# A four-direction scan block: both directions streamed side by side, the short convolution as banded matmuls on column tiles

## The chip, the cores and the metric

One NeuronCore of a Trainium2 chip runs the whole program. The metric is the device time of one execution in microseconds. TensorE (PE in the profile) multiplies, VectorE (DVE) and ScalarE (ACT) do elementwise work, GpSimd (POOL) does elementwise work on SBUF, and SyncE (SP) issues most DMAs.

## The reference

The input is 4 images of 128 channels and 96 x 96 pixels, float32. Each is group-normalised (32 groups of 4 channels, mean and variance over the whole image), read as a sequence of 9216 pixels in four orders (by lines forward and reversed, by columns forward and reversed), and each sequence goes through the same small network:

```python
t = _grouped1x1(x, in_proj_w, in_proj_b, G)          # 4 groups of 32 channels -> 128 each
u, gate = (t[:, :HID], t[:, HID:])                   # 256 channels each
u = jax.nn.silu(u)
u = lax.conv_general_dilated(u, dw_w, ..., feature_group_count=HID)   # 5 taps, per channel
s = _conv1x1(u, ssm_in_w)                            # 256 -> 32
a = DMIN + (DMAX - DMIN) * jax.nn.sigmoid(_conv1x1(u, ssm_delta_w, ssm_delta_b))
a = jnp.clip(a, 0.0001, 0.9999)
bb = jnp.tanh(_conv1x1(u, ssm_b_w, ssm_b_b))
cc = jnp.tanh(_conv1x1(u, ssm_c_w, ssm_c_b))
prefix = jnp.cumsum(jnp.log(a), axis=-1)
hst = jnp.exp(prefix) * jnp.cumsum(bb * s * jnp.exp(-prefix), axis=-1)  # h = a h + bb s
u = u + _conv1x1(cc * hst + ssm_d[None, :, None] * s, ssm_out_w)        # 32 -> 256
u = _grouped1x1(u * jax.nn.sigmoid(gate), mix_w, mix_b, G)
return _conv1x1(u, out_proj_w, out_proj_b)           # 256 -> 128
```

The four results go back to the pixel order, are fused by a 512-to-128 product, and the input is added. So 4 x 4 x 9216 = 147456 pixels pass through the network.

## The kernel before

All data is float32, channels on partitions, pixels along the free dimension. An image is read in a column order (V, from a transposed copy in memory) and then a line order (H): 8 phases. `xn` holds the normalised image of the phase, `sil` the activated first half of the input product for the whole image (two halves of 128 channels, two pixels of padding at each end), and `acc` the input plus all results so far. Mix, output and fuse products are folded at the start into one matrix per direction and half, `w_fin`.

A phase makes two passes over the image, one per direction; the reversed one takes the taps mirrored and the scan backwards. A pass has 20 chunks: 18 of 5 lines (480 pixels) and 2 of 3 lines (288). The main loop runs over 8 x 2 x 20 = 320 steps in program order, and each engine works through its own instructions in that order:

- `conv_and_gate` (lines 240 to 277): for the first 128 channels five matmuls with diagonal matrices (`diag`), accumulated in PSUM (`pc`); for the others one ACT copy with a scale and four DVE multiply-adds; then the gate's two matmuls on 32 rows each (`pg`) and their sigmoid.
- `ssm_out` of the step before (lines 321 to 331): two matmuls of 32 rows (`z` into `pc` and `pz`), and the product with the gate on DVE.
- `front` (lines 207 to 238) for a chunk of the next phase, in the second pass only: normalisation, two matmuls of 32 rows (`pu`), sigmoid, and the product that makes it a silu, stored in `sil`. So one front serves both passes.
- `scan` (lines 281 to 319): two matmuls (`pp`, 4 x 32 outputs: s, b, c, delta), three activations, two POOL operations on `a`, and DVE's product, scan and two more operations, all on 32 partitions.
- `accumulate` of the step before (lines 333 to 358): two matmuls (`py`) and the addition into `acc`; on the last pass of an image the chunk is written out and the next image's chunk is loaded into `acc`.

Statistics of the next image (`stats_chunk`, `stats_finish`) run in the first V pass. PSUM has 8 banks: two each for `ps_x` (front and gate), `ps_u`, `ps_p`, one each for `ps_z` and `ps_y`.

## Time and profile before

| | |
|---|---|
| times of three runs | 3605.2, 3606.55, 3615.43 us (median 3606.55) |
| the profiled execution | 3603.76 us, its span 3602.0 us |
| mean granted TensorE clock | 0.945 |
| instructions | 27637 |
| DMA | 92.14 MB, mean 26 GB/s |

The span runs from the first to the last instruction that the profiler recorded. In the views of the profile, PE is matmuls and PEld weight loads; a group is given by line, engine and operation, out<-in by the program's names, out and in as partitions x elements, the count, then busy us and mean ns of one, then the idle time of the engine just before and what released it. In a timeline a row is start (us), length (us), engine, line, operation and count of what is merged in it.

### The profile page before, as it was taken

The numbers are of one execution on the slowest core, as the hardware profiler recorded it, in microseconds if no ns is written. First come the engines' busy times: TensorE is split into PE (matmuls) and PEld (weight loads), VectorE is DVE, ScalarE is ACT, GpSimd is POOL, SyncE is SP. The second block draws the span as 40 slices with busy tenths as digits, with TensorE's granted clock in tenths as the row PEclk, the third lists the DMA queues.
The fourth block names the chain that finished last, engine by engine and source line by source line (L and its number), as shares of the span: only waits on it lengthen the run. The fifth ranks groups of instructions, "written<-read, shape, count | busy, mean of one in ns | idle before, by whom it ended". The sixth has DMA issues, their size and how long they took to land.

```text
span 3602.0 us, 27637 instructions
## 1 busy us (share of the span) xinstructions
PE 3501.1 (97%) x9032; PEld 1539.4 (43%) x9032; DVE 2877.5 (80%) x4442; ACT 1572.0 (44%) x2572; POOL 393.0 (11%) x653
## 2 busy tenths in 40 slices
PE   7999999999999999999999999999999999999999
PEld 3334444444444444444444444444444444444443
DVE  7888887788877888778887788777887788877777
ACT  3334444444444444344444444444444344444343
POOL 0011111111111111111111111111111111111111
PEclk7899999999999999999999999999999999999999
DMA  4210000011200000001110000000120000000000
GB/s 151 86 34 15 20 20 1 0 39 58 62 0 0 18 22 14 1 0 54 59 46 0 4 20 22 9 0 6 58 66 29 0 7 22 20 6 0 6 22 26
DMA packets 56625, 92.14 MB, mean 26 GB/s; under 512 B 7296, under 2 KB 56352, under 8 KB 56480
## 3 DMA queue, kind: packets, MB, share of 16 engines
q1 hardware_dynamic: 54720, 89.68, 8.2%
q8 instruction: 70, 1.15, 0.1%
q10 hardware_dynamic: 1760, 0.70, 0.1%
q14 instruction: 75, 0.61, 0.1%
HBM read 71.48 MB, written 18.87 MB: 25 GB/s over the span
## 4 chain that ended last, share of the span: by engine, by line
PE 44%; DVE 44%; issue 6%; ACT 4%; DMA 2%; ACTq 0%; POOL 0%; DVEq 0%; POOLq 0%
DVE u L261 12%; PE pc L248 11%; PE pc L324 8%; PE pp L287 8%; DVE h L308 7%; PE pz L328 6%; PE py L339 5%; DVE z L318 4%; DVE tb L302 4%; DVE z L317 4%; DVE gv L331 3%; DVE u L330 3%; PE pu L224 3%; PE pg L270 3%; ACT u L259 3%
## 5 line engine op out<-in xcount | busy, mean ns | idle before, releaser
L248 PE MATMUL pc<-sil,diag 128*128 128x480 f32 (+1 forms) x3200 | 1298.1, 552 | 0.0
L261 DVE SCALAR_TENSOR_TENSOR u<-sil,w_dw,u 128x480 f32<-128x480 f32 (+1 forms) x1280 | 889.0, 695 | 135.5 <-ACT u L259 124.0
L248 PEld LDWEIGHTS pc<-sil,diag 128*128 128x128 f32 x3200 | 609.9, 191 | 641.0 <-issue 623.0
L287 PE MATMUL pp<-u,w_proj 128*128 128x480 f32 (+1 forms) x1280 | 698.8, 674 | 2.8 <-DVE u L261 2.2
L264 ACT COPY u<-pc 128x480 f32<-128x480 f32 (+1 forms) x320 | 173.8, 543 | 1046.1 <-PE pc L248 1046.0
L339 PE MATMUL py<-gv,w_fin 128*128 128x480 f32 (+1 forms) x1280 | 588.9, 584 | 1.0
L300 POOL TENSOR_SCALAR a<-a 32x480 f32<-32x480 f32 (+1 forms) x320 | 190.9, 597 | 3173.1 <-ACT a L294 3173.1
L329 DVE TENSOR_TENSOR gv<-pc,gv 128x480 f32<-128x480 f32 (+1 forms) x320 | 204.0, 638 | 344.1 <-PE pc L324 335.5
L274 ACT ACTIVATE gv<-pg,b_in 128x480 f32<-128x480 f32 (+1 forms) x640 | 379.2, 642 | 143.3 <-PE pg L270 132.1
L287 PEld LDWEIGHTS pp<-u,w_proj 128*128 128x128 f32 x1280 | 247.0, 215 | 386.1 <-issue 269.5
L339 PEld LDWEIGHTS py<-gv,w_fin 128*128 128x128 f32 x1280 | 270.6, 213 | 311.5 <-issue 226.7
L324 PE MATMUL pc<-z,w_so 32*128 32x480 f32 (+1 forms) x640 | 332.1, 598 | 64.6 <-DVE z L318 62.7
L259 ACT ACTIVATE u<-sil,w_dw 128x480 f32<-128x480 f32 (+1 forms) x320 | 216.7, 677 | 382.2 <-DVE gv L331 376.3
L308 DVE TENSOR_TENSOR_SCAN h<-a,h,tb 32x480 f32<-32x480 f32 (+1 forms) x304 | 354.6, 1167 | 2.1 <-POOL a L301 1.0
L270 PE MATMUL pg<-xn,w_in 32*128 32x480 f32 (+1 forms) x1280 | 345.5, 600 | 0.6 <-ACT gv L274 0.6
L228 ACT ACTIVATE sg<-pu,b_in 128x480 f32<-128x480 f32 (+1 forms) x320 | 202.1, 639 | 258.9 <-PE pu L224 258.7
L328 PE MATMUL pz<-z,w_so 32*128 32x480 f32 (+1 forms) x640 | 300.8, 549 | 0.0
L292 ACT ACTIVATE tb<-pp,b_proj 32x480 f32<-32x480 f32 (+1 forms) x320 | 204.0, 637 | 142.3 <-PE pp L287 136.6
L224 PE MATMUL pu<-xn,w_in 32*128 32x480 f32 (+1 forms) x640 | 251.0, 625 | 10.2 <-DVE sil L231 7.9
L302 DVE TENSOR_TENSOR tb<-pp,tb 32x480 f32<-32x480 f32 (+1 forms) x320 | 199.1, 622 | 73.5 <-ACT z L298 71.6
L330 DVE TENSOR_TENSOR u<-pz,u 128x480 f32<-128x480 f32 (+1 forms) x320 | 203.9, 637 | 42.7 <-PE pz L328 2.1
L231 DVE SCALAR_TENSOR_TENSOR sil<-pu,b_in,sg 128x480 f32<-128x480 f32 (+1 forms) x320 | 219.5, 692 | 21.7 <-ACT sg L228 19.8
(54 smaller groups left out, 2050.0 us busy)
## 6 DMA issues: line engine op xcount, KB each, us to landing
xn<-in_xv SPq DMA_DIRECT2D x72, 240.0 KB, 2.6
acc<-in_xh SPq DMA_DIRECT2D x72, 240.0 KB, 2.8
xn<-in_xh SPq DMA_DIRECT2D x72, 240.0 KB, 2.6
out<-res SPq DMA_DIRECT2D x72, 240.0 KB, 2.0
xs<-in_xh SPq DMA_DIRECT2D x54, 240.0 KB, 2.6
xn<-in_xv SPq DMA_DIRECT2D x8, 144.0 KB, 2.3
acc<-in_xh SPq DMA_DIRECT2D x8, 144.0 KB, 2.3
xn<-in_xh SPq DMA_DIRECT2D x8, 144.0 KB, 2.1
```

The lines of the kernel that those rows point to most:

```text
L224: nc.tensor.matmul(pt[:, :n], w_in[q, :], xn[q, span(c)], start=True, stop=True)
L248: nc.tensor.matmul(pu[:, :n], diag[:, w, :], sil[:, 0, bass.ds(o + k, n)], start=(k == 0), stop=(k == K - 1),)
L259: nc.scalar.activation(u[:, 1, :n], src, AF.Copy, scale=coef)
L261: nc.vector.scalar_tensor_tensor(u[:, 1, :n], src, coef, u[:, 1, :n], ALU.mult, ALU.add)
L270: nc.tensor.matmul(pg[:, :n], w_in[q, :], xn[q, span(c)], start=True, stop=True)
L274: nc.scalar.activation(gv[:, j, :n], pgs[j][:, :n], AF.Sigmoid, bias=b_in[:, 2 + j : 3 + j])
L287: nc.tensor.matmul(pp[:, :n], w_proj[:, j, :], u[:, j, :n], start=(j == 1), stop=(j == 0))
L302: nc.vector.tensor_mul(tb[:, :n], s, tb[:, :n])
L308: nc.vector.tensor_tensor_scan(dirn(h), dirn(a), dirn(tb), 0.0 if st["first"] else carry[0], ALU.mult, ALU.add,)
L324: nc.tensor.matmul(pu[:, :n], w_so[:, 0:P], z[:, :n], start=False, stop=True, skip_group_check=True)
L328: nc.tensor.matmul(pz[:, :n], w_so[:, P:HID], z[:, :n], start=True, stop=True)
L339: nc.tensor.matmul(py[:, :n], w_fin[:, d, j, :], gv[:, j, :n], start=(j == 0), stop=(j == 1))
```

## The change

The layouts in memory change: `xs` holds the four sequences of each image already in their order, padded, and with every fourth pixel together (pixel 4n + q stands at [q, n]); `xr` holds the images in line order with the same split within a line, and so do `acc` and the output.

Both directions of a phase now advance together. A stretch is 16 lines (1536 pixels) of each direction's own sequence, and a unit is one of its four pixel phases p (384 pixels, every fourth one) of one direction s: 8 phases x 6 stretches x 4 x 2 = 384 units, with s alternating. `sil` for the whole image, `xn` and the normalised copy are gone: `wn` and `bn` carry the normalisation in weights and biases, front is computed anew for each direction, and only `x_in` (two input tiles) and a double-buffered `sil` per direction remain.

- `rows` does the front of one channel group g (32 channels of both halves, four pixel phases stacked on 4 x 32 partitions) eight units ahead, the gate of the unit eleven units back, and the product out of the scan (`pz`) for that unit; silu is one ACT operation, sigmoids become tanh with the halves moved into weights.
- `conv` contracts over 4 pixels x 32 channels: for each half, block k and group g a matmul of 128 rows and 32 columns with a banded matrix (`band`). DVE and the diagonal matmuls have no part in it any more.
- `proj` serves a pair of units (both directions of one p): call 0 gives b and delta, call 1 gives c and s, each for two directions on 4 x 32 columns; so the products, the scan (one of 1536 columns on 64 partitions per stretch) and the output products work on both directions at once.
- `accumulate` reverses the result of the second direction as it adds. After the last unit of a stretch, 16 lines of `acc` are written out and loaded with the next image.

Every matmul in these functions writes 32 columns (`mm`, column tile `col`). PSUM has four banks for `x` (front, gate, conv, `py`), two for `z`, one each for `p0` and `p1`.

```diff
-LINES = [5] * 18 + [3] * 2
...
+R = 4
+LN = 16
+NS = HH // LN
+N = LN * WW // R
+M = WW // R
+LAG = 11
+UB = 8
...
-    xn = big.tile([P, L], F32, name="xn")
-    sil = big.tile([P, 2, L + 2 * PAD], F32, name="sil")
+    x_in = [big.tile([P, R, N + 1], F32, name=f"x_in{s}") for s in range(2)]
...
+    phases = [
+        (b, order, dirs)
+        for b in range(B)
+        for order, dirs in (("V", ((0, 2), (1, 3))), ("H", ((2, 0), (3, 1))))
+    ]
...
+    def psx(name):
+        return ps.tile([P, 512], F32, tag="x", bufs=4, name=name)
...
+        wn = sp.tile([P, P], F32, tag="wn", name=f"wn_{b}")
+        nc.vector.tensor_scalar_mul(wn, w_in, norm[:, 1:2])
+        gm4 = sp.tile([P, 4], F32, tag="gm4", name=f"gm4_{b}")
+        nc.vector.tensor_scalar_mul(gm4, gmask, norm[:, 0:1])
+        pb = psx(f"pbn_{b}")
+        nc.tensor.matmul(pb[:, 0:4], wn, gm4, start=True, stop=True)
+        bn = sp.tile([P, 4], F32, tag="bnorm", name=f"bnorm_{b}")
+        nc.vector.tensor_sub(bn, b_in, pb[:, 0:4])
+        nc.vector.tensor_scalar_mul(bn[:, 2:4], bn[:, 2:4], 0.5)
+        bs = sp.tile([P, 2, 4], F32, tag="bsilu", name=f"bsilu_{b}")
+        for q in range(R):
+            for g in range(4):
+                nc.gpsimd.tensor_copy(
+                    bs[32 * q : 32 * q + 32, :, g], bn[32 * g : 32 * g + 32, 0:2]
+                )
+        stats[b] = (wn, bn, bs)
...
+    def load_front(step, s):
+        if step * UB < NU:
+            un = units[step * UB + s]
+            nc.sync.dma_start(
+                x_in[s][0:64, :, :],
+                xs[un["b"], un["lay"], 0:64, :, bass.ds(un["st"] * N, N + 1)],
+            )
+    def gate_at(un):
+        return (un["p"] + PAD) % R, (un["p"] + PAD) // R
+    def load_gate(i):
+        if i < NU:
+            un = units[i]
+            q, _ = gate_at(un)
+            nc.sync.dma_start(
+                x_in[un["s"]][64:P, q, :],
+                xs[un["b"], un["lay"], 64:P, q, bass.ds(un["st"] * N, N + 1)],
+            )
...
+        for q in range(R):
+            r = slice(32 * q, 32 * q + 32)
+            nc.gpsimd.tensor_copy(id32[r, :], ident[r, r])
+        for j in range(2):
+            for p in range(R):
+                for k in range(2):
+                    for g in range(4):
+                        m = R * k - p + R - 1
+                        nc.gpsimd.tensor_scalar_mul(
+                            band[:, j, p, k, g, :], id32, w_dw[:, j, g, m : m + 1]
+                        )
...
-                nc.vector.tensor_copy(w_fin[:, d, j, :], pt[:, :P])
+                nc.vector.tensor_scalar_mul(w_fin[:, d, j, :], pt[:, :P], 0.5)
...
-    def front(ph, c): ...
-    def conv_and_gate(st): ...
-    def scan(st): ...
-    def ssm_out(st): ...
-    def accumulate(st): ...
+    def mm(o, col, lhsT, rhs, start, stop):
+        r = slice(32 * col, 32 * col + 32)
+        nc.tensor.matmul(o[r, : rhs.shape[-1]], lhsT, rhs, start=start, stop=stop,
+                         skip_group_check=True)
+    sils = {}
+    def rows(i, bi):
+        front = gate = None
+        if i is not None:
+            step, k = divmod(i, UB)
+            s, g = divmod(k, 4)
+            un = units[step * UB + s]
+            wn, _, bsil = stats[un["b"]]
+            if g == 0:
+                sils[step, s] = wk.tile(
+                    [P, 2, 4, N + 1], F32, tag=f"sil{s}", name=f"sil_{step}_{s}"
+                )
+            sil = sils[step, s]
+            pf = [psx(f"pf_{i}_{j}") for j in range(2)]
+            front = (un, wn, bsil, s, g, sil, pf)
+        if bi is not None:
+            bu = units[bi]
+            gwn, gbn, _ = stats[bu["b"]]
+            pg = [psx(f"pg_{bu['id']}_{j}") for j in range(2)]
+            gate = (bu, gwn, gbn, pg)
+        for c in range(4):
+            if front:
+                for j in range(2):
+                    r = slice(32 * j, 32 * j + 32)
+                    mm(pf[j], c, wn[r, 32 * g : 32 * g + 32], x_in[s][r, c, :], True, True)
+            if gate:
+                q, off = gate_at(bu)
+                for j in range(2):
+                    r = slice(64 + 32 * j, 96 + 32 * j)
+                    mm(pg[j], c, gwn[r, 32 * c : 32 * c + 32],
+                       x_in[bu["s"]][r, q, off : off + N], True, True)
+        if gate:
+            pz = ps.tile([P, 2, 512], F32, tag="z", name=f"pz_{bu['id']}")
+            z = scans[bu["step"]][1]
+            for c in range(4):
+                for j in range(2):
+                    r = slice(64 * j + 32 * bu["s"], 64 * j + 32 * bu["s"] + 32)
+                    mm(pz[:, j, :], c, w_so[r, 128 * j + 32 * c : 128 * j + 32 * c + 32],
+                       z[r, bu["p"], :], True, True)
+        if front:
+            for j in range(2):
+                nc.scalar.activation(
+                    sil[:, j, g, :], pf[j][:, : N + 1], AF.Silu, bias=bsil[:, j, g : g + 1]
+                )
+            if g == 3:
+                if un["st"] == 0:
+                    nc.gpsimd.memset(sil[0:64, :, :, 0:1], 0.0)
+                if un["st"] == NS - 1:
+                    nc.gpsimd.memset(sil[64:P, :, :, N : N + 1], 0.0)
+                load_front(step + 1, s)
+        if gate:
+            gv = wk.tile([P, 2, N], F32, tag="gv", name=f"gv_{bu['id']}")
+            for j in range(2):
+                nc.scalar.activation(
+                    gv[:, j, :], pg[j][:, :N], AF.Tanh, bias=gbn[:, 2 + j : 3 + j], scale=0.5
+                )
+            load_gate(bi + UB)
+            u = bu["u"]
+            nc.vector.tensor_add(pz[:, :, :N], pz[:, :, :N], u)
+            nc.vector.scalar_tensor_tensor(gv, gv, 1.0, pz[:, :, :N], ALU.add, ALU.mult)
+            bu["v"] = gv
+    def conv(un, j):
+        sil = sils[un["step"], un["s"]]
+        if j == 0:
+            un["u"] = wk.tile([P, 2, N], F32, tag="u", bufs=LAG, name=f"u_{un['id']}")
+        pc = psx(f"pc_{un['id']}_{j}")
+        for k in range(2):
+            for g in range(4):
+                mm(pc, g, band[:, j, un["p"], k, g, :], sil[:, j, g, k : k + N], k == 0, k == 1)
+        nc.scalar.copy(un["u"][:, j, :], pc[:, :N])
+    scans = {}
+    qb, qc, qa, qs = (slice(MH * i, MH * (i + 1)) for i in range(4))
+    def proj(i, which):
+        un = units[i]
+        step, p = un["step"], un["p"]
+        if step not in scans:
+            scans[step] = [
+                wk.tile([P, N, R], F32, tag="t0", name=f"t0_{step}").rearrange("p n r -> p r n"),
+                wk.tile([P, R, N], F32, tag="t1", name=f"t1_{step}"),
+            ]
+        ta, tb = scans[step]
+        pp = ps.tile([P, 512], F32, tag=f"p{which}", name=f"pp_{un['id']}_{which}")
+        cols = (qb, qb, qa, qa) if which == 0 else (qc, qc, qs, qs)
+        for j in range(2):
+            for c in range(4):
+                mm(pp, c, w_proj[:, j, cols[c]], units[i + c % 2]["u"][:, j, :], j == 0, j == 1)
+        if which == 0:
+            nc.scalar.activation(ta[:, p, :], pp[:, :N], AF.Tanh, bias=b_proj[:, 0:1])
+            a = ta[64:P, p, :]
+            half = (DMAX - DMIN) / 2
+            nc.gpsimd.tensor_scalar(a, a, half, DMIN + half, ALU.mult, ALU.add)
+            nc.gpsimd.tensor_scalar(a, a, 0.9999, 0.0001, ALU.min, ALU.max)
+        else:
+            nc.scalar.activation(
+                tb[0:64, p, :], pp[0:64, :N], AF.Tanh, bias=b_proj[0:64, 1:2]
+            )
+            un["pp"] = pp
+    def products(i):
+        un = units[i]
+        (ta, tb), p, pp = scans[un["step"]], un["p"], un["pp"]
+        nc.vector.tensor_mul(ta[0:64, p, :], pp[64:P, :N], ta[0:64, p, :])
+        nc.vector.tensor_scalar_mul(tb[64:P, p, :], pp[64:P, :N], d_sb[64:P, :])
+    def scan(step):
+        ta = scans[step][0]
+        seq = ta.rearrange("p r n -> p (n r)")
+        first = units[step * UB]["st"] == 0
+        init = 0.0 if first else scans[step - 1][0][0:64, R - 1, N - 1 : N]
+        nc.vector.tensor_tensor_scan(
+            seq[0:64], seq[64:P], seq[0:64], init, ALU.mult, ALU.add
+        )
+    def outputs(step, p):
+        ta, tb = scans[step]
+        nc.vector.tensor_mul(tb[0:64, p, :], tb[0:64, p, :], ta[0:64, p, :])
+        nc.vector.tensor_add(tb[64:P, p, :], tb[0:64, p, :], tb[64:P, p, :])
+        nc.gpsimd.tensor_copy(tb[0:64, p, :], tb[64:P, p, :])
+    def accumulate(bu):
+        b, s, p, st = bu["b"], bu["s"], bu["p"], bu["st"]
+        py = psx(f"py_{bu['id']}")
+        for j in range(2):
+            for c in range(4):
+                mm(py, c, w_fin[:, bu["dir"], j, 32 * c : 32 * c + 32], bu["v"][:, j, :],
+                   j == 0, j == 1)
+        y = py[:, :N]
+        if s:
+            y, p, st = y[:, ::-1], R - 1 - p, NS - 1 - st
+        if bu["order"] == "V":
+            part = acc.rearrange("p (m q) r c -> p m q r c", q=R)[
+                :, :, p, :, bass.ds(st * LN // R, LN // R)
+            ]
+            y = y.rearrange("p (c r m) -> p m r c", r=R, m=M)
+            nc.vector.tensor_add(part, y, part)
+            return
+        part = acc[:, bass.ts(st, LN), p, :]
+        y = y.rearrange("p (h m) -> p h m", m=M)
+        if s == 0:
+            nc.vector.scalar_tensor_tensor(part, y, b_fin, part, ALU.add, ALU.add)
+        else:
+            nc.vector.tensor_add(part, y, part)
+        if bu["st"] >= NS // 2 and bu["p"] == R - 1:
+            r = bass.ts(st, LN * WW)
+            nc.sync.dma_start(out[b, :, r], accf[:, r])
+            if b + 1 < B:
+                nc.sync.dma_start(accf[:, r], xr[b + 1, :, r])
+    stats_finish(b0)
+    for i in range(UB):
+        rows(i, None)
+    for t in range(NU + LAG + 1):
+        bi = t - LAG
+        if t >= 3 and t % 2 and t - 3 < NU:
+            products(t - 3)
+        rows(t + UB if t + UB < NU else None, bi if 0 <= bi < NU else None)
+        if t < NU:
+            conv(units[t], 0)
+        if 0 <= bi - 1 < NU:
+            accumulate(units[bi - 1])
+        if t < NU:
+            conv(units[t], 1)
+            un = units[t]
+            if un["order"] == "V" and t % 2 == 0 and un["b"] + 1 < B:
+                stats_chunk(un["b"] + 1, (un["st"] * UB + un["k"]) // 2)
+                if un["st"] == NS - 1 and un["k"] == UB - 2:
+                    stats_finish(un["b"] + 1)
+        if t % 2 and t < NU:
+            proj(t - 1, 0)
+        elif t % 2 == 0 and 2 <= t <= NU:
+            proj(t - 2, 1)
+        if t >= UB + 1 and t % UB == 1 and t - UB - 1 < NU:
+            scan(t // UB - 1)
+        if t >= UB + 1 and t % 2 and t - UB - 1 < NU:
+            d = units[t - UB - 1]
+            outputs(d["step"], d["p"])
```

318 lines of the change are left out of this document (88 added, 230 removed).

## The prediction

> **What bounds the kernel now.** I read the page's busy lines first, then the chain of waits, then the groups by line with shapes kept apart, then a stretch of the timeline in the steady part.
>
> ```profile
> PE 3501.1 (97%) x9032; PEld 1539.4 (43%) x9032; DVE 2877.5 (80%) x4442; ACT 1572.0 (44%) x2572; POOL 393.0 (11%) x653
> ...
> PEclk7899999999999999999999999999999999999999
> ...
> PE 44%; DVE 44%; issue 6%; ACT 4%; DMA 2%; ACTq 0%; POOL 0%; DVEq 0%; POOLq 0%
> ```
>
> PE is busy for 97% of 3602.0 us; the chain alternates between PE and DVE because each waits for the other once per step, but only PE has no room left. Is this PE time real streaming or idle pipeline? The groups and the timeline say streaming:
>
> ```profile
> L248 PE MATMUL pc<-sil,diag 128*128 128x480 f32 x2880 | 1210.7, 567 | 0.0
> ...
> L287 PE MATMUL pp<-u,w_proj 128*128 128x480 f32 x1152 | 651.3, 696 | 0.1
> ...
> L270 PE MATMUL pg<-xn,w_in 32*128 32x480 f32 x1152 | 317.4, 616 | 0.0
> ...
> L248 PE MATMUL pc<-sil,diag 128*128 128x288 f32 x320 | 87.4, 417 | 0.0
> ```
> ```profile
> 999.81 2.18 PE L248 MATMUL pc<-sil,diag 128*128 128x480 f32 x5
> ...
> 1000.21 0.19 PEld L248 LDWEIGHTS pc<-sil,diag 128*128 128x128 f32 x1 [0.21 <-issue]
> ...
> 1001.91 0.30 PEld L270 LDWEIGHTS pg<-xn,w_in 32*128 32x128 f32 x4 [0.70 <-DVE h L308]
> 1001.92 1.07 PE L270 MATMUL pg<-xn,w_in 32*128 32x480 f32 x4
> ...
> 1004.59 1.88 PE L287 MATMUL pp<-u,w_proj 128*128 128x480 f32 x4
> ```
>
> Each matmul in the code is two records (3200 records for 5 taps in 320 steps), so one matmul is two passes. Five conv passes take 2.18 us, the last one by the group's mean 0.567 long: (2.18 - 0.567)/4 = 403 ns from start to start. Over the whole run a conv pass costs 1210.7/2880 = 420 ns, since the granted clock is not always full. The weight loads lie under the passes (0.19 us each, one at 1000.21 inside the run of matmuls). So a pass that follows another costs 420 ns for 480 columns, and a step costs passes: 14 matmuls, 28 of them. (The means of 567 to 696 ns hold the pipeline's tail, which the next pass covers.)
>
> One thing decides this case. The four passes of the projection use all 128 rows and take 1.88 us; the four of the gate use rows 64-95 and 96-127 and take 1.07 us, and over the run 1152 of the one are 651.3 us of PE, 1152 of the other 317.4: two tiles of the array ran side by side. The trace of before has this for row tiles; it has nothing that writes fewer than 128 columns, so nothing on column tiles.
>
> **The change part by part: PE.** The unit of work is now 384 columns instead of a step of 480 (or 288): 8 phases x 6 stretches x 4 pixel phases x 2 directions = 384 units. A pass of 384 columns by the two conv rows: in proportion 420 x 384/480 = 336 ns; on the line between 420 (480) and 87.4/320 = 273 (288) it is 347 ns. I take 340 and call it a slot. All matmuls have 32 output columns now, so four of them fill what one filled before, if they run side by side. Slots per unit, with four at once:
> - front and gate: 16 matmuls of 32 rows x 32 columns on 16 different tiles, two passes: 2 slots. Before: 3 matmuls on average per step.
> - out of the scan (pz): 8 matmuls on two row tiles x four column tiles: 2 slots. They use row tiles that front has just used, so I don't let them overlap it.
> - conv: 2 halves x 2 blocks x 4 groups = 16 matmuls, two passes each, 32/4 = 8 slots. Before: 5 taps for 128 of the 256 channels on PE (10 passes), the others on DVE. The band covers both halves in 8 slots.
> - projection: two calls per pair of units, each 2 halves x 4 column tiles, so 8 matmuls per unit, 16/4 = 4 slots.
> - final product (py): 8 matmuls, 4 slots.
>
> Sum 20 slots x 0.340 = 6.8 us. Two changes of tile form per unit come on top (32-row tiles to 128-row tiles and back). Their price is in these rows:
>
> ```profile
> 1001.42 0.56 PE L248 MATMUL pc<-sil,diag 128*128 128x480 f32 x1
> ...
> 1002.79 0.67 PE L324 MATMUL pc<-z,w_so 32*128 32x480 f32 x1
> ```
>
> From the last conv pass at 1001.42 to the gate at 1001.92 are 0.50 us instead of 0.40, and a first pass after such a wait lasts 0.67 instead of 0.56 because its weight load shows: 0.2 us per change, 0.4 per unit.
>
> **Waits on PE.** Four PSUM buffers serve front, gate, conv and py in a ring, seven allocations per unit. The conv of a unit takes the buffer of its front, so it waits for one Silu: ready at 0.7 us plus some 0.2, done at 1.5; conv could start at 2+2 slots plus 0.2 = 1.56. About even. The projection of every second unit needs the copy of the conv just ended (0.2 + 0.48 us), with two slots of the other half ahead of it: under 0.1 us per unit. I take 0.1 for both. Unit: 6.8 + 0.4 + 0.1 = 7.3 us; 384 of them 2803 us.
>
> **The other engines** must fit in 7.3 us.
>
> ```profile
> L274 ACT ACTIVATE gv<-pg,b_in 128x480 f32<-128x480 f32 x576 | 349.9, 657 | 128.5 <-PE pg L270 126.2 <-PE pc L324 2.2
> L308 DVE TENSOR_TENSOR_SCAN h<-a,h,tb 32x480 f32<-32x480 f32 x280 | 335.4, 1198 | 0.7
> ...
> L329 DVE TENSOR_TENSOR gv<-pc,gv 128x480 f32<-128x480 f32 x288 | 189.4, 658 | 323.9 <-PE pc L324 322.2 <-ACT gv L274 1.7
> ...
> L300 POOL TENSOR_SCALAR a<-a 32x480 f32<-32x480 f32 x288 | 175.5, 609 | 2931.9 <-ACT a L294 2931.9
> ...
> L294 ACT ACT_TABLE_LOAD x3 | 3.8, 1283 | 0.1
> ```
>
> These are for 480 columns; 384 can't cost more, nor less than 384/480 = 0.8 of it. ACT: two Silu, two Tanh for the gate, one Tanh for the projection and two copies, 7 x 0.657 = 4.6 us a unit at most, 3.7 at least. If Silu and Tanh share no table, two loads of 1.28 us make it 7.2, just inside. DVE: add and gate product over 768 columns each, 2 x 1.6 x 0.658 = 2.1; accumulate 0.66; four products on 64 partitions per pair, 1.3 a unit; the scan of 1536 columns, both directions in one, 3.2 x 1.198 = 3.8 us per eight units, 0.5: 4.6 us at most, 4.0 with the 0.8 on the short ones. The four conv operations of DVE are gone, and the normalisation with them. POOL: two scalings and a copy per pair, 0.6 each: 0.9 a unit. All of it is hidden by PE; if PE cost nothing, DVE would set the end at 384 x 4.3 = 1.65 ms.
>
> SP issues a gate load per unit and a front load per four or so, each needed 5 to 8 units (36 us and more) later; a DMA of 240 KB lands in 2 us (below), so they cost nothing unless more than 36 us stand ahead of them in the queue.
>
> **What lies around the units.**
>
> ```profile
> GB/s 151 86 34 15 20 20 1 0 39 58 62 0 0 18 22 14 1 0 54 59 46 0 4 20 22 9 0 6 58 66 29 0 7 22 20 6 0 6 22 26
> ...
> out<-res SPq DMA_DIRECT2D x72, 240.0 KB, 2.0
> ```
> ```profile
> 27.58 1.95 PE L201 MATMUL pb<-b_mix,w_of 128*128 128x1 f32 x16
> ...
> 33.69 1.97 PE L224 MATMUL pu<-xn,w_in 32*128 32x480 f32 x4 [1.11 <-DVE xn L212]
> ```
>
> Before, the first front matmul starts at 33.69 us. The image still has to be read whole for its statistics; then come a longer chain that folds the normalisation into weights, and eight fronts at two Silu each (10 us): the first conv at about 50. The last write is 10 us. At the three borders of images, the first V unit adds into all lines of the accumulator, so it waits for the last 16 lines to be written out and read again, now in 786 KB pieces: 5.2 us each at the 151 GB/s of the first slice, two after one another, some 2 us of landing, less one unit of slack: 6 us, three times. Before it was 240 KB pieces (2.0 us). The statistics of the next image stand in PE's program order and wait there for DVE and ACT: about 7 us, three times. Together 50 + 10 + 18 + 21 = 100, with 10 for the uneven edges 110 us. Span 2803 + 110 = 2913; the profiled execution of before is 3603.76 us for a span of 3602.0, so **2915 us**. The median of the runs shown, 3606.55, stands 3 us above that execution, which is nothing here.
>
> **Bounds of what the trace does not show.** Fewest slots: pz beside front, 18 slots, 6.6 us, 2650 us. No two column tiles at once: 64 passes on full rows plus 16, 80 slots, 27.7 us, 10.7 ms. Between them I take four at once, since the row tiles of the gate, the nearest rows, overlap fully. The clock: 403 of 420 ns is a share of 0.96; at 1.0 a unit is 0.27 us shorter (-105 us), at 0.85 it is 0.88 longer (+340 us).
>
> The Trainium skill, TensorE: Matmul & The Clock Gate, section Part 3: Packing small matmuls — row/col tiling, reports a speedup of 2.38 for three column tiles; taken as 0.79 of full side-by-side work, the 16 slots on full rows become 20.2, and an estimate by that page is 8.7 us a unit, 3.46 ms. No run so far shows column tiles, so the sum doesn't use it.
>
> **Rivals.**
> - *Column tiles start in program order.* A matmul's second pass must wait for its first on the same tile. If the next column tile waits behind it, only two passes overlap: n matmuls take n + 1 slots. Full-row work is 32 matmuls, 33 slots; front/gate and pz 5 + 5 (row tiles free, as the gate row shows): 43 slots, 14.6 + 0.5 us, 5.8 + 0.11 = **5.9 ms, slower**. The place is conv, py and projection; it decides as soon as fewer than three of four run at once: (3606 - 110)/384 = 9.1 us a unit, less 0.5 and 4 slots leaves 7.2 us for 64 passes of 0.34, which is 3.0 at once. For it: the trace has no column tile. Against it: in the gate row, program order would give starts at 0, 0.4, 0.4, 0.8 and so 1.4 us, not 1.07. The same page and section state that matmuls start and end in program order; this trace's row tiles disagree, no run so far shows column tiles, and by that rule this rival holds. Chance 0.12.
> - *PE is bound by issue.* A unit has 112 loads and 112 matmuls where a step had 28 of each. The shortest pairs in the trace, one column wide, come every 1.95/16 = 122 ns; 112 x 0.122 = 13.7 us, **5.4 ms**. Against: those loads are four times as wide, and four gate loads start within 0.30 us. Chance 0.06.
> - *Three of four at once*, the loads of the tiles getting in each other's way: 16 slots become 21.3, 9.1 us, 3.6 ms, from 3.4 to 4.0. Chance 0.11, half of it on each side.
> - *A wait in place of streaming:* the PSUM ring and the single buffers of pz and the projections make PE wait for ACT and, after a 3.8 us scan, for DVE; Silu unhidden 0.6, copy 0.1, scan 3.8/8: 1.2 us a unit, 8.5, **3.4 ms**. For it: PE and DVE take turns in 44% each of the chain already. Against: DVE and ACT have over 2.5 us of room per unit. Chance 0.12.
>
> **How the numbers follow.** The forecast, 2650 to 3250, has 0.57; below it 0.02. About 0.3% is what a measurement of this kernel tells from no change. Faster: 0.57 + 0.02 + 0.12 + 0.05 = 0.76; the same 0.01; slower 0.12 + 0.06 + 0.05 = 0.23. From 2650 to 4000 lies 0.80; the forecast's own range is 2650 to 3250.
>
> **What would show it.** Starts of four conv matmuls of one block a few ns apart, then a pause of 0.32 to 0.35 us, show the column tiles; a start every 80 ns evenly would do as well; pairs every 0.34 us show the in-order rival, an even 120 ns the issue rival. PE busy near 95% with DVE near 55% and ACT between 45 and 60% shows the unit; PE idle before conv with a Silu as releaser shows the wait. Three gaps of 6 us before V accumulates and three of 7 at the statistics show the borders. The forecast is wrong above all if columns don't overlap.

## The result and the profile after

The changed kernel takes 3055.94 us (median of 4 runs, 3052.45 to 3061.32) against 3609.11 us (3605.2 to 3615.43), a ratio of 0.8467 [0.8449, 0.8486]. The forecast was 2915 us: right in direction, 141 us or 5% low. The profiled execution of after has a span of 3053.0 us at a mean granted clock of 0.977 (before 3602.0 us at 0.945). Busy lines, clock and chain of after, from its page:

```profile
PE 2884.2 (94%) x43088; PEld 1082.3 (35%) x43088; DVE 1728.2 (57%) x2119; ACT 1440.5 (47%) x2703; POOL 526.9 (17%) x754
...
PEclk9999999999999999999999999999999999999999
...
PE 79%; DVE 14%; DMA 4%; ACT 2%; issue 1%; SPq 0%; ACTq 0%; DVEq 0%
```

PE now stands for most of the chain, as the forecast had it, but DVE still ends 14% of it, in a kernel where DVE was to be hidden. First the plain unit, in the timeline of PE (start, length, engine, line, operation, count):

```profile
1499.52 1.11 PE L300 MATMUL pz<-t,w_so 32*32 32x384 f32 x16
1500.57 1.50 PE L300 MATMUL pc<-sil,band 128*32 128x384 f32 x16
1501.88 1.47 PE L300 MATMUL py<-gv,w_fin 128*32 128x384 f32 x16
1503.17 1.48 PE L300 MATMUL pc<-sil,band 128*32 128x384 f32 x16
1504.46 1.47 PE L300 MATMUL pp<-u,w_proj 128*32 128x384 f32 x16
1505.86 0.51 PE L300 MATMUL pf<-x_in,wn 32*32 32x385 f32 x2
```

Sixteen passes on all rows take 1.29 us from start to start (1501.88, 1503.17, 1504.46): 0.322 us for four, and a single pass of full width takes as long (e3 below). Inside such a row the records start four at a time, 7 ns apart, with a pause of 0.32 us behind them: the sign that the prediction named. So the column tiles run four at once, at no loss. From `pz` at 1499.52 to conv at 1500.57 are 1.05 us, of which two slots are 0.64: the change from 32-row to 128-row tiles costs 0.40 (e8 tells it from a wait for the Silu).

Now the unit at the border of a stretch, where a scan runs. The timelines of DVE, ACT and PE, in that order, and then the busy time by windows (length; PE, PEld, DVE, ACT, POOL busy with counts; granted clock; DMA):

```profile
852.47 0.87 DVE L411 TENSOR_TENSOR t<-pp,t 64x384 f32<-64x384 f32 x1 [2.57 <-ACT t L403]
853.37 0.62 DVE L412 TENSOR_SCALAR t<-pp,d_sb 64x384 f32<-64x384 f32 x1
854.03 3.35 DVE L419 TENSOR_TENSOR_SCAN t<-t 64x1536 f32<-64x1536 f32 x1
857.41 1.59 DVE L425 TENSOR_TENSOR t<-t,t 64x384 f32<-64x384 f32 x2
859.03 0.97 DVE L364 TENSOR_TENSOR pz<-pz,u 128x768 f32<-128x768 f32 x1
```
```profile
860.09 0.86 ACT L376 COPY u<-pc 128x384 f32<-128x384 f32 x2 [5.29 <-DVE pz L364]
```
```profile
857.34 0.81 PE L300 MATMUL pp<-u,w_proj 128*32 128x384 f32 x2
860.62 2.78 PE L300 MATMUL pp<-u,w_proj 128*32 128x384 f32 x14 [2.47 <-ACT u L376]
```
```profile
857.50:860.60 3.10, 0.65 (x6) 0.00 (x0) 3.02 (x4) 0.51 (x2) 0.00 (x0) 0.95 0.00 0
860.60:864.00 3.40, 3.38 (x41) 1.12 (x47) 3.29 (x5) 0.83 (x2) 1.70 (x2) 0.54 0.00 0
864.00:868.00 4.00, 4.00 (x84) 1.58 (x55) 3.55 (x5) 3.00 (x6) 3.21 (x4) 1.00 0.09 29
```

DVE does a pair's products, the scan and two output products in one run of 6.4 us, and only then the addition `pz` + u (L364) of the next unit. ACT's copy of the new u waits for it 5.29 us, because the copy takes over the buffer that the addition reads. PE has issued its first two passes of `pp`, which read a u already there, and stands for 2.47 us. Then the clock falls to half (0.54 over the next 3.4 us): fourteen passes take 2.78 us where sixteen took 1.47. The waits of after, summed over the span (us in total, times, longest):

```profile
ACT u L376 <- DVE pz L364: 337.5, 194, 14.7
...
PEld pp L300 <- ACT u L376: 174.7, 101, 7.1
...
PE pp L300 <- ACT u L376: 121.2, 48, 6.4
```

The last line has 48 waits, all but a few of them 2.5 us long and at the border of a stretch. From scan to scan are 61.4 us (median), while eight plain units of 7.095 (7.02 and 7.17 in turn) are 56.8. So 4.6 us a stretch are lost, some 223 us in all: more than the whole miss.

### The profile page after: what moved, and what is told of

Read it like the earlier page. It is cut to its first block, busy times and chain, and to the rows that moved or that the text cites. A ratio compares the mean times of both kernels' runs of the same rounds, so it can differ in the third digit from the quotient of the medians.

```text
span 3053.0 us, 95151 instructions
## 1 busy us (share of the span) xinstructions
PE 2884.2 (94%) x43088; PEld 1082.3 (35%) x43088; DVE 1728.2 (57%) x2119; ACT 1440.5 (47%) x2703; POOL 526.9 (17%) x754
## 4 chain that ended last, share of the span: by engine, by line
PE 79%; DVE 14%; DMA 4%; ACT 2%; issue 1%; SPq 0%; ACTq 0%; DVEq 0%
PE pc L300 28%; PE pp L300 18%; PE py L300 14%; PE pz L300 9%; PE pf L300 8%; DVE t L419 5%; DMA xs<-in_xr 3%; DVE t L425 3%; PE pg L300 2%; DVE pz L364 2%; DVE t L411 1%; DVE t L412 1%; ACT t L403 1%; ACT u L376 1%; DVE bn L296 1%
## 5 line engine op out<-in xcount | busy, mean ns | idle before, releaser
L300 PE MATMUL pc<-sil,band 128*32 128x384 f32 x12288 | 1148.4, 490 | 0.5
L300 PE MATMUL pp<-u,w_proj 128*32 128x384 f32 x6144 | 676.2, 512 | 124.3 <-ACT u L376 121.2
L364 DVE TENSOR_TENSOR pz<-pz,u 128x768 f32<-128x768 f32 x384 | 370.7, 965 | 548.6 <-PE pz L300 542.7
L300 PEld LDWEIGHTS pc<-sil,band 128*32 128x32 f32 x12288 | 366.7, 109 | 686.3 <-issue 404.1
L300 PE MATMUL py<-gv,w_fin 128*32 128x384 f32 x6144 | 570.3, 488 | 0.7 <-DVE gv L365 0.7
L300 PE MATMUL pz<-t,w_so 32*32 32x384 f32 x6144 | 445.9, 495 | 10.9 <-DVE gv L365 6.0
L347 ACT ACTIVATE sil<-pf,bsilu 128x385 f32<-128x385 f32 x768 | 405.4, 579 | 95.0 <-PE pg L300 89.7
L359 ACT ACTIVATE gv<-pg,bnorm 128x384 f32<-128x384 f32 x768 | 405.3, 587 | 29.5 <-PE pg L300 29.5
L365 DVE SCALAR_TENSOR_TENSOR gv<-gv,pz 128x768 f32<-128x768 f32 x384 | 366.5, 954 | 73.2 <-ACT gv L359 54.0
L300 PE MATMUL pf<-x_in,wn 32*32 32x385 f32 x6144 | 384.9, 512 | 2.4 <-ACT u L376 1.2
L397 ACT ACTIVATE t<-pp,b_proj 128x384 f32<-128x384 f32 x192 | 203.2, 1058 | 237.8 <-PE pp L300 237.8
```

The source lines that it names most:

```text
L300: nc.tensor.matmul(o[r, : rhs.shape[-1]], lhsT, rhs, start=start, stop=stop, skip_group_check=True)
L347: nc.scalar.activation(sil[:, j, g, :], pf[j][:, : N + 1], AF.Silu, bias=bsil[:, j, g : g + 1])
L359: nc.scalar.activation(gv[:, j, :], pg[j][:, :N], AF.Tanh, bias=gbn[:, 2 + j : 3 + j], scale=0.5)
L364: nc.vector.tensor_add(pz[:, :, :N], pz[:, :, :N], u)
L365: nc.vector.scalar_tensor_tensor(gv, gv, 1.0, pz[:, :, :N], ALU.add, ALU.mult)
L397: nc.scalar.activation(ta[:, p, :], pp[:, :N], AF.Tanh, bias=b_proj[:, 0:1])
```

## The experiments

Theory A says that the buffer is at fault (u held too long); theory B that the order in DVE's queue is (scan and output products ahead of the additions). Two more runs test the column tiles against the rivals that stand in the prediction.

**e1: two more buffers for u.**

```diff
-            un["u"] = wk.tile([P, 2, N], F32, tag="u", bufs=LAG, name=f"u_{un['id']}")
+            un["u"] = wk.tile([P, 2, N], F32, tag="u", bufs=LAG + 2, name=f"u_{un['id']}")
```

> The u buffers go from 11 to 13. In the changed kernel one unit per stretch lasts 11.7 us instead of 7.1 (46 of them, some 200 us), and its long wait reads: PE's projection for ACT's copy of u, that copy for DVE's add of pz and u, that add behind the scan. Theory A (the lifetime of u): the copy waits only because with 11 buffers it overwrites the u that the add of the same step still reads; with 13 the copy runs at once, the long units shrink to about 7.5 and the time falls by 150 to 200 us, to 2860-2905. Theory B (the queue of DVE): products, scan and two output products, 6.4 us, stand ahead of the add, and the add, the gate product and the accumulation are late for the PSUM buffers of pz and py as well; then PE waits for DVE's accumulation or gate product in place of ACT's copy, and the time falls by under 60 us, to 3000-3056.

Measured 3145.79 us, 0.872 [0.8707, 0.8733]: 90 us slower than after. The longest waits of PE in e1:

```profile
PE pg L300 <- DVE acc L444: 90.9, 30, 3.9
PE pg L300 <- DVE acc L451: 70.2, 21, 4.0
```

The copy no longer waits, but PE now waits for the next thing behind the scan on DVE: the addition into `acc` (L444, L451), which frees the PSUM buffer that the gate's `pg` wants. 48 pieces of 2.5 us have become 51 of 3.2, and the granted clock is 0.949. The clock alone takes (1 - 0.949) x 3147 = 160 us against (1 - 0.977) x 3053 = 70 us, as much more as the whole difference. Theory A falls. Theory B had named this wait, but had a gain of up to 60 us for it; that the kernel would become slower neither had foreseen.

**e2: the scan and the output products placed behind the additions on DVE**, with all buffers as in after.

```diff
+            ins = accumulate(units[bi - 1])
+            after = partial(tc.issue_after, ins.ins)
...
-                scan(t // UB - 1)
+            with after():
+                scan(t // UB - 1)
...
-            outputs(d["step"], d["p"])
+            with after():
+                outputs(d["step"], d["p"])
```

> The scan and the output products are queued on DVE behind the accumulation of their step, in the order of the program, instead of ahead of the add of pz and u. u keeps 11 buffers. Theory B (the order of DVE's queue): the add is on time, the scan falls into DVE's idle time of 2 to 3 us per unit, and the long units nearly go: 150 to 200 us less, 2860-2905. Theory A (the lifetime of u alone): the copy of the next step still waits for an add that now stands behind scan and outputs, by 1 to 2 us; 46 x 1.5 = 70 us remain, so 2920-2990. If neither holds (the scan's length itself, wherever it stands): 3056 within 1%.

Measured 2891.24 us, 0.8014 [0.8002, 0.8026], clock 0.995, 57.9 us from scan to scan. The timelines of DVE, ACT and PE at a border of e2, in that order (lines one higher than in after):

```profile
1048.11 0.97 DVE L365 TENSOR_TENSOR pz<-pz,u 128x768 f32<-128x768 f32 x1
1049.18 0.95 DVE L366 SCALAR_TENSOR_TENSOR gv<-gv,pz 128x768 f32<-128x768 f32 x1
1050.40 0.56 DVE L445 TENSOR_TENSOR acc<-py,acc 128x384 f32<-128x384 f32 x1 [0.27 <-PE py L301]
1050.99 3.41 DVE L420 TENSOR_TENSOR_SCAN t<-t,t 64x1536 f32<-64x1536 f32 x1
1054.44 0.83 DVE L426 TENSOR_TENSOR t<-t,t 64x384 f32<-64x384 f32 x1
```
```profile
1054.50 0.93 ACT L398 ACTIVATE t<-pp,b_proj 128x384 f32<-128x384 f32 x1 [2.33 <-DVE t L420]
```
```profile
1055.83 1.50 PE L301 MATMUL pc<-sil,band 128*32 128x384 f32 x16 [1.04 <-ACT sil L348]
```

The additions go first, the scan and the output products after them. 165 us came back with one change of order and no change of work: theory B holds. What is left of the border, 1.1 us, is the scan still: ACT's next tanh (L398) waits 2.33 us for it, the Silu behind that tanh is late, and the conv waits for the Silu.

**e5: both edits together**, to see whether the buffers matter once the order is right.

> Both edits: 13 buffers of u, and scan and output products behind the accumulation. With the order alone a stretch lasts 57.9 us against 56.8 for eight plain units; what is left is conv waiting for Silu for 1.3 us once per stretch (39.7 us in 38 waits), and ACT is late there because its copy of u still waits for DVE's add. If that is the lifetime of u (theory A as the smaller half of the stall), 13 buffers now take it away: 45 to 55 us less, 2836-2846. If DVE's queue holds PE by itself there too, nothing changes: 2891 within 0.5%. More buffers alone cost 90 us, all of it by the granted clock (0.949): if buffers as such slow PE, this one is slower than 2891.

Measured 2888.93 us, 0.8008 [0.7996, 0.802]: e2 within 0.1%. The buffers of u don't matter.

**e3: the final product as two matmuls of 128 columns instead of eight of 32.**

```diff
-            for c in range(4):
-                mm(py, c, w_fin[:, bu["dir"], j, 32 * c : 32 * c + 32], bu["v"][:, j, :],
-                   j == 0, j == 1)
+            nc.tensor.matmul(py[:, :N], w_fin[:, bu["dir"], j, :], bu["v"][:, j, :],
+                             start=j == 0, stop=j == 1)
```

> The final product is computed by two matmuls of 128 columns in place of eight of 32 columns; everything else is as in the changed kernel. Four column tiles at once and one full width should cost the same 4 slots. If each change of tile form drains the array whatever the form (0.2 us by the row changes of the kernel before), two more changes per unit add 0.4 x 384 = 150 us: 3200. If only a change of the number of rows costs, or if column tiles cost as much as full width without any loss: 3056 within 0.5%. If column tiles themselves lose something (loads or starts of four tiles), it is faster: 3000 or below.

Measured 3161.29 us, 0.8758 [0.8744, 0.8773]: slower by 105 us, at the same granted clock (0.979). PE's timeline in e3:

```profile
1505.35 1.50 PE L300 MATMUL pc<-sil,band 128*32 128x384 f32 x16
1506.78 1.56 PE L433 MATMUL py<-gv,w_fin 128*128 128x384 f32 x4
1508.26 1.50 PE L300 MATMUL pc<-sil,band 128*32 128x384 f32 x16
```

Four passes of full width take 1.48 us where sixteen narrow ones take 1.29, and the conv ahead of them 1.43 instead of 1.31. The full passes behind the first start 0.322 us apart, as four narrow ones do. So side-by-side work costs nothing against full width, and a change of tile form costs 0.12 us one way and 0.19 the other even where the rows stay the same: 0.3 x 384 = 115 us a run, near the 105 measured.

**e4: in conv, the two blocks of one column tile one after the other**, so that program order holds four passes of the same tile in a row.

```diff
-        for k in range(2):
-            for g in range(4):
+        for g in range(4):
+            for k in range(2):
```

> The conv's loops are exchanged: the two blocks of one column tile follow one another, then the next tile, so that in program order four passes of one tile stand in a row. If each column tile has its own queue and PE looks 32 loads and matmuls ahead: no change, 3056 within 0.5%. If matmuls start in program order and only neighbours overlap: 13 slots instead of 4 per half, 5.8 us more per unit, 5.3 ms. In between, a limited window: 3.2 to 4 ms.

Measured 3062.55 us, 0.849 [0.8477, 0.8502], 0.2% from after. PE's timeline in e4:

```profile
1507.20 1.52 PE L300 MATMUL pc<-sil,band 128*32 128x384 f32 x16
1508.52 1.49 PE L300 MATMUL py<-gv,w_fin 128*32 128x384 f32 x16
```

The conv still takes 1.32 us, and its records again start four at a time, 13 ns apart, with 0.32 us between the fours. If tiles started in program order, three quarters of the overlap would be gone. Each tile has its own order.

**e7: one intermediate tile laid out without a stride.** `t0`, on which tanh, POOL's scalings, the products and the scan work, holds the four pixel phases interleaved, so all but the scan step through it by 16 bytes. Here each phase is contiguous (the scan then runs over the pixels of a stretch in another order).

```diff
-                wk.tile([P, N, R], F32, tag="t0", name=f"t0_{step}").rearrange("p n r -> p r n"),
+                wk.tile([P, R, N], F32, tag="t0", name=f"t0_{step}"),
...
-        seq = ta.rearrange("p r n -> p (n r)")
+        seq = ta.rearrange("p r n -> p (r n)")
```

> The tile t0 is contiguous per pixel phase and the scan runs through it in that order, so the scan's order of pixels is left out; the number and size of operations is that of the changed kernel. Theory: a step of 16 bytes between elements is what makes ACT's tanh into t0 last 1.06 us instead of 0.58, DVE's products 0.88 and 0.85 instead of 0.56 and POOL's scalings 0.94 instead of 0.55; all of them fall to the shorter figure. The border of a stretch then holds 0.9 us less of DVE work ahead of the add (products 0.32, two output products 0.58), the long units get 0.9 us shorter: 48 x 0.9 = 43 us, and with fewer windows of half clock up to 60: 2995-3015. Rival: these lengths come from other causes (DVE and POOL sharing SBUF, 128 or 64 partitions); then they stay and so does the time, 3056 within 0.5%.

Measured 2987.75 us, 0.8283 [0.827, 0.8297], clock 0.995. The groups by line (busy, mean ns of one, idle before) of after, and then of e7:

```profile
L397 ACT ACTIVATE t<-pp,b_proj 128x384 f32<-128x384 f32 x192 | 203.2, 1058 | 237.8 <-PE pp L300 237.8
...
L400 POOL TENSOR_SCALAR t<-t 64x384 f32<-64x384 f32 x192 | 180.8, 942 | 1534.5 <-ACT t L397 1530.7
...
L411 DVE TENSOR_TENSOR t<-pp,t 64x384 f32<-64x384 f32 x192 | 169.2, 881 | 461.1 <-ACT t L403 460.8
```
```profile
L397 ACT ACTIVATE t<-pp,b_proj 128x384 f32<-128x384 f32 x192 | 111.6, 581 | 200.2 <-PE pp L300 200.2
...
L411 DVE TENSOR_TENSOR t<-pp,t 64x384 f32<-64x384 f32 x192 | 107.2, 559 | 462.0 <-ACT t L403 461.8
...
L400 POOL TENSOR_SCALAR t<-t 64x384 f32<-64x384 f32 x192 | 98.4, 513 | 1609.8 <-ACT t L397 1605.9
```

The stride makes these 1.6 to 1.8 times as long. Without it DVE's run ahead of the addition is 0.32 + 2 x 0.30 = 0.9 us shorter, 43 us over 48 borders (PE's wait for u fell from 121.2 to 79.2 us in all); and after the shorter stalls the clock falls less often, (1 - 0.995) x 2988 = 15 us lost for 70. The 68 us measured lie between the 43 and the sum of both. This edit and e2 act on the same run of DVE; they were not tried together.

**e8: e5 with the projections in one PSUM bank and the bank so freed given to the ring of `x`.**

```diff
-        return ps.tile([P, 512], F32, tag="x", bufs=4, name=name)
+        return ps.tile([P, 512], F32, tag="x", bufs=5, name=name)
...
-        pp = ps.tile([P, 512], F32, tag=f"p{which}", name=f"pp_{un['id']}_{which}")
+        pp = ps.tile([P, 512], F32, tag="p", name=f"pp_{un['id']}_{which}")
```

> Both edits of the order and of u, and one bank for the projections in place of two, which gives the PSUM ring of front, gate, conv and final product a fifth buffer. In the plain unit conv starts 1.05 us after pz where two slots and a change of form are 0.85: 0.2 us are the wait for Silu on the buffer that conv takes over. If the ring is the cause: 0.2 x 384 = 75 us less than with four buffers, 2765-2775. If the change of tile form is dearer than thought and Silu is not late, nothing changes: 2840 within 0.5%. If one bank for the projections is too few (ACT and DVE still read it), PE waits there and it is slower.

Measured **2836.99 us, 0.7864 [0.7852, 0.7875]**, the fastest of all. The gain of 52 us isn't in the plain unit, where `pz` to conv still takes 1043 ns. In 38 units of e8 the Silu ends 2.13 us after `pz` starts, and conv starts at the same 1.04 us: so that time is the change of form and no wait for a Silu. The gain is at the borders, where e5 had this wait left and e8 has none (waits of PE in e5):

```profile
PE pc L301 <- ACT sil L348: 39.4, 38, 1.0
```

From scan to scan e8 needs 56.8 us, eight plain units and nothing else. (Two edits at once, not tried apart; but with the Silu as late as before and the conv no longer waiting for it, it is the larger ring that this gain needs.)

**e9: e8 without the second block of the conv** (half of its matmuls), to see what the next bound is.

> The kernel of the five-buffer run (2837 us) without the second block of the conv: half of the conv's products are left out. 8 of 32 passes per column tile and unit go: 4 slots of 0.322 us, 1.29 us a unit, 495 us in all if PE's slots set the end everywhere: 2340-2350. If ACT, DVE or the PSUM ring take over once a unit is 5.8 us (ACT has 4.3 us of work per unit, DVE 4.5), the gain is smaller: 2400-2600. If PE was not the bound, nothing: 2837 within 1%.

Measured 2443.69 us, 0.6773 [0.6757, 0.6789], clock 0.98: 393 us less than e8. Eight slots were four, 4 x 0.322 x 384 = 495 us of streaming; 102 of them did not come: DVE (70% busy in e9) and ACT then hold PE back in places, and the clock is lower. So PE is the bound in e8, and of 1.29 us taken out of its unit 1.02 come back before the others count.

**e12: e8 with the second conv of a unit ahead of `accumulate`**, so that `py` covers the copy of u.

```diff
+        if t < NU:
+            conv(units[t], 1)
         if 0 <= bi - 1 < NU:
             ins = accumulate(units[bi - 1])
             after = partial(tc.issue_after, ins.ins)
-            conv(units[t], 1)
```

> The version with the later scan, projections of one bank and five conv buffers (2837 us), with the second conv block of a unit issued ahead of the first one's accumulation and py products, so that the copy of u by ACT has the py passes as its cover. All of the computation is done. Theory: the 0.15 us that PE waits for u in every second unit goes, 0.076 x 384 = 29 us: about 2808 us. Rival: the wait for u has only changed places with a later one (the products of py reach the accumulation later, the ring of conv buffers is held longer): 2837 us or a few per cent above it.

Measured 2876.18 us, 0.7966 [0.7953, 0.7979]: 39 us slower than e8. The theory's part came true: all plain units take 7.02 us instead of 7.02 and 7.17 in turn. The rival's part is the larger. ACT's and PE's timelines of e12 at a border:

```profile
1055.14 0.94 ACT L398 ACTIVATE t<-pp,b_proj 128x384 f32<-128x384 f32 x1 [4.91 <-DVE t L420]
1055.88 1.01 ACT L348 ACTIVATE sil<-pf,bsilu 128x385 f32<-128x385 f32 x2
```
```profile
1053.92 1.50 PE L301 MATMUL pc<-sil,band 128*32 128x384 f32 x16
1056.47 1.50 PE L301 MATMUL pc<-sil,band 128*32 128x384 f32 x16 [1.05 <-ACT sil L348]
```

`py` comes later, so the addition, the scan behind it, and the tanh that writes over what the scan reads (L398) come later too; the Silu queued behind that tanh on ACT is then late for the conv. 38 borders of 48 have such a unit, 1.25 us longer: 48 us lost for 28 won, the rest in a few longer waits. The same lesson as in e1: the long run on DVE reaches PE through whatever stands next behind it.

**e10, e11 and e13: what bounded the kernel before.** e10 is the kernel before with one of the four multiply-adds of VectorE (three taps of the second half left out), e11 with four of the five diagonal matmuls (one tap left out), e13 with both cuts. (The expectation of e13 calls the first cut "one left out"; three of the four are, as in e10.)

```diff
-            else:
+            elif k == 1:
                 nc.vector.scalar_tensor_tensor(
```
```diff
-        for k, w in taps:
+        for k, w in taps[:4]:
...
-                stop=(k == K - 1),
+                stop=(k == K - 2),
```

> The kernel before, without three of the four multiply-adds of DVE per step (three taps of the second half of the channels are left out): 960 operations of 0.7 us, 670 us of DVE's 2877. If only PE's streaming bounds the kernel before, the time stays: 3606 within 1%. If the 44% that DVE has of the chain of waits are a cost of their own, it falls by up to 300 us and more.

> The kernel before, without the fifth diagonal matmul per step (one tap of the first half of the channels is left out): 2 of 28 passes. If PE's slots bound it, 640 passes of 0.40 us go: 250 us less, 3355. If DVE, with 80% of the span busy, takes over at once: 3500-3600.

> The kernel before with both cuts together: one of the four multiply-adds of VectorE left out (three taps of the second half are not computed) and four of the five diagonal matmuls (one more tap left out). Theory: in the kernel before, PE lost time to VectorE, and each wait brought half clock; so with VectorE relieved the two fewer passes a part that made the kernel slower by 224 us now pay what they save as streaming, about 250 us: about 3070 us, with a granted clock near 0.97. Rival: less TensorE work lowers the clock by itself, whoever PE waits for: no gain on the 3321 us of the VectorE cut alone, and a clock below 0.95.

| | us | ratio to before | clock | PEld `pc` waits for DVE z (L318) |
|---|---|---|---|---|
| before | 3609 | 1 | 0.945 | 270.9 us |
| e10 | 3321.34 | 0.9202 [0.9172, 0.9232] | 0.975 | 37.2 us |
| e11 | 3833.12 | 1.062 [1.0571, 1.067] | 0.878 | 422.5 us |
| e13 | 3286.89 | 0.9114 [0.9099, 0.913] | 0.945 | 217.7 us |

Less work for DVE gave 288 us; less work for PE cost 224, where both branches of its expectation had a gain. PE's timeline in before, and then in e11:

```profile
1509.43 1.07 PE L270 MATMUL pg<-xn,w_in 32*128 32x480 f32 x4
...
1519.69 1.07 PE L270 MATMUL pg<-xn,w_in 32*128 32x480 f32 x4
1520.94 1.07 PE L324 MATMUL pc<-z,w_so 32*128 32x480 f32 x2 [0.17 <-DVE z L318]
...
1530.18 1.07 PE L270 MATMUL pg<-xn,w_in 32*128 32x480 f32 x4
```
```profile
1514.25 1.07 PE L270 MATMUL pg<-xn,w_in 32*128 32x480 f32 x4
...
1524.52 1.07 PE L270 MATMUL pg<-xn,w_in 32*128 32x480 f32 x4
1526.57 1.07 PE L324 MATMUL pc<-z,w_so 32*128 32x480 f32 x2 [0.98 <-DVE z L318]
...
1535.01 1.07 PE L270 MATMUL pg<-xn,w_in 32*128 32x480 f32 x4
```

Steps of 10.26 and 10.49 us in before, 10.27 and 10.49 in e11, with two passes (0.8 us) fewer: PE only waits 0.8 us longer for z. The step is set by a round through both engines: `py` on PE, then acc, product, scan and two operations on DVE up to z, between them the multiply-adds, then PE's `pc`, then DVE again. DVE's timeline of before shows the round without a gap from the multiply-adds to z, and with short waits for ACT and PE elsewhere:

```profile
1514.53 1.47 DVE L261 SCALAR_TENSOR_TENSOR u<-sil,w_dw,u 128x480 f32<-128x480 f32 x2 [0.82 <-ACT u L259]
...
1520.18 0.70 DVE L318 SCALAR_TENSOR_TENSOR z<-pp,d_sb,z 32x480 f32<-32x480 f32 x1
1522.04 0.66 DVE L329 TENSOR_TENSOR gv<-pc,gv 128x480 f32<-128x480 f32 x1 [1.16 <-PE pc L324]
```

The 224 us lie in the clock: (1 - 0.878) x 3818 = 466 us lost against 198 in before, 268 more. That the longer waits bring it is an inference: in the 3.41 us ahead of e11's half-clock stretches PE's records have 0.75 us of idle time (median), ahead of full clock none.

e13 is neither theory's. Its time and clock are near the rival's numbers (35 us below e10, clock 0.945). At full clock its steps of 480 columns with a front in them take 10.08 us against 10.64 in e10 (means, from gate to gate), which is most of the 0.8 that two passes are worth; those without a front take 9.29 against 9.50, held by the round again, with the wait of `pc`'s weight loads for z back at 217.7 us. And 61 of 161 of these run into half clock, 3 of 161 in e10: half clock costs e13 181 us and e10 83. So the theory that DVE's load alone was the other bound falls: it is the round, whose length the multiply-adds only added to. Whether fewer passes lower the clock by themselves, as the rival has it, stays open: PE's records show next to no idle time (median 0.04 us) in the 3.41 us ahead of e13's half-clock stretches. That no other order could open the round wasn't tried.

## Why the prediction was right or wrong

| term | predicted | measured in after |
|---|---|---|
| slot | 0.340 us x 20 = 6.8 | 0.322 x 20 = 6.44 |
| changes of form | 0.4 | 0.40 + 0.11, and 0.06 of small gaps |
| waits in the plain unit | 0.1 | 0.08, u's copy alone |
| plain unit, x 384 | 7.3, 2803 us | 7.095, 2724 us |
| borders of stretches | 0 | 48 x 4.6 = 223 us |
| around the units | 110 us | 106 us (rest of the span) |
| span | 2913 us | 3053 us |

- *What was right:* the slots. Four column tiles at once, 20 slots, the form change and the wait for u's copy in every second unit all stand in the timeline. The slot was oversized by 5%, since 420 ns was a mean with half clock in it and a full stretch has 403 ns for 480 columns: 0.36 us a unit, 138 us. The change back to 32 rows and the small gaps gave 0.17 us of it back, so that the plain units came out 79 us too high.
- *Luck:* that excess of 79 us hid a third of the 223 us at the borders, which the sum had at nothing. The miss of 141 us looks smaller than the step that failed.
- *The step that failed: "All of it is hidden by PE".* DVE's sum of 4.0 to 4.6 us a unit was right (1728.2/384 = 4.5). But it is a mean, and a queue isn't a mean: at a border DVE has 6.4 us in one piece in front of an addition that PE needs through u. The sum counted the scan as load, 0.5 us a unit, and held the room of 2.5 us a unit against the rival that let it stall PE. It needed the question what is queued behind the scan, and how soon that is wanted. e2 shows that the room was there: with the addition first, the loss is gone but for 1.1 us a border.
- *POOL "0.6 each"* was 0.94 with a 16-byte step (e7), and ACT's tanh 1.06 rather than 0.66: "384 can't cost more" left the step out. Off the path in the plain unit, on it at the borders.
- *The first step, "only PE has no room left",* was a wrong reading of before. e10 and e11 show a round through DVE and PE; PE's 97% held tails and half clock (the 44% each of the chain pointed at the round). The sum didn't suffer, because it was built from the new unit and not from what before would lose. But a forecast by passes removed would have failed: two passes fewer made before slower. That DVE lost its conv I booked as hidden; taking 960 of these operations out of before alone gave 288 us.
- *The rivals.* Program order and three at once: refuted by the 0.322 us and by e4. The Trainium skill (TensorE: Matmul & The Clock Gate, Part 3: Packing small matmuls — row/col tiling) has matmuls start and end strictly in program order, and a speedup of 2.38 for three column tiles; both differ from this trace, where four column tiles in a steady stream do four times the work of one (0.322 us for four passes). Issue-bound: refuted, 16 passes in 1.29 us are 80 ns each. Waits in place of streaming: its term for the scan, 3.8/8 us a unit or 182 us, was near and belonged in the sum (223 us measured); its Silu of 0.6 us a unit, the larger half, is not waited for in the plain unit (e8), so its 3.4 ms was wrong.
- *Around the units:* at the borders of images DVE waits 3.8 us each for the lines of `acc` (predicted 6), of which 0.9 to 1.8 us reach the stretch's length; the statistics cost about 4.5 (7); the first conv starts at 49.4 us (50).

## What to carry to other kernels

A mean load per unit says that an engine can keep up, not that it does: look in each engine's queue for the longest piece that runs at once, and for what stands behind it and who wants that. Order is then the cheapest cure (165 us here), while more buffers may only pass the wait on to the next instruction behind the same piece. Before counting what fewer passes on PE bring, find the round that sets the step, and see whether PE only fills it.

## What was not expected of the hardware

- *Half clock after short stalls, and without them.* The granted clock is 1.0 or 0.5, and its half stretches last 3.41 us or a multiple, on one fixed grid (they start at 860.31, 925.16 and 1048.04 us in after: 19 and 36 times 3.413 apart). In after, PE had stood idle for 2.1 to 2.4 us (middle half of the cases) of the 3.41 us ahead of a half-clock stretch; of the other pieces of the grid 99% had less than 1.7 us. The Trainium skill (TensorE: Matmul & The Clock Gate, What's actually happening) names a window of about 3.4 us, which agrees, and an idle window as the cause; in after a window idle for two thirds was enough. In before the middle half of such pieces has 0.2 to 0.4 us of idle time, and in e13 the median is 0.04 us: idle time in PE's records isn't the measure alone, and what else counts stays open.
- *A 16-byte step in SBUF* costs ACT 1058 against 581 ns, DVE 881 against 559, POOL 942 against 513; the scan, contiguous in one case and the other, is 3.41 us in both. The Trainium skill (SBUF — State Buffer, Door 1: The DMA port swizzle) gives lines of 16 bytes that need two hits for full bandwidth; the trace agrees, as every element here is on a line of its own.
- *Column tiles have queues of their own* (e4), and a change of the tile's form has a price of its own: 0.40 us from 32 to 128 rows, 0.12 and 0.19 us between 32 and 128 columns (e3).
